# Second group norm's statistics from the spectrum, block by block, and the last tile's columns transformed by halves

## The chip, the cores and the metric

One core of a Trainium2 chip runs the whole program. The time is the device time of one execution in microseconds (us), and lower is better. The core has a matrix engine (PE, TensorE, with its weight loads listed as PEld), a vector engine (DVE), an activation engine (ACT, ScalarE), a general engine (POOL, GpSimd) and a sync engine (SP) that here issues all DMA transfers. Each engine works through its own instructions in order and waits on semaphores for the others.

## What is computed

The input x has shape (2, 48, 48, 768), all in 32-bit floats. Two layers with residuals are applied:

```python
x = x + attention(_gn(x), ...)      # layer 0: 12 heads, relative positions
x = x + spectral(_gn(x), ...)       # layer 1

def _gn(v, G=32, eps=1e-5):         # per image and per group of 24 channels
    g = v.reshape(B_, H_, W_, G, C_ // G)
    m = jnp.mean(g, axis=(1, 2, 4), keepdims=True)
    s = jnp.var(g, axis=(1, 2, 4), keepdims=True)
    return ((g - m) / jnp.sqrt(s + eps)).reshape(v.shape)

# layer 1
xf = jnp.fft.rfft2(x, axes=(1, 2), norm='ortho')
o1r, o1i = gelu(complex block-diagonal product of xf with w1, plus b1)  # 8 blocks of 96 channels
o2r, o2i = softshrink(complex block-diagonal product with w2, plus b2)
out = jnp.fft.irfft2(o2r + 1j * o2i, s=(H, W), axes=(1, 2), norm='ortho')
```

The change concerns the second `_gn`. Its mean only shifts the constant term of the transform, and its division by the deviation can be put into the rows of w1, because the transform is linear. The transform is orthonormal, so the sum of squares over the spectrum equals the sum of squares over the tokens; of a real input only 25 of 48 columns are kept, so the columns 1 to 23 count twice.

## The kernel before, in words

The two images (index b) are treated one after the other by the same code: first `attention`, then `project_out`, then `Spectral.run`. In the profiled execution `project_out` of the first image runs from about 1473 to 1662 us and its spectral part to about 1920 us; of the second image from about 3388 to 3580 us and to the end.

**Order of the work.** Inside attention, each engine's order is written out by hand (`InOrder`, which is why its lines appear as L67). In `project_out` and `Spectral` nothing is pinned: a scheduler lays out each engine's instructions ahead of the run. It takes the instruction that comes first in the code among those that it reckons to be ready, so an instruction from later code can stand before one from earlier code. On the chip each engine then keeps to that order.

**`project_out`** (L641). The result of attention lies in DRAM as oT. It is loaded three tiles of 128 tokens at a time (`Projection.tokens`, L623: one load of oT at L631, two loads of the softmax's inverses at L633 into one buffer `inv`, and one multiplication on POOL at L637). There are two buffers for the loaded group, so group g + 2 waits for the matmuls of group g. The residual x is loaded in six parts of 384 tokens (L653), and POOL adds the bias to each of their 24 rows (L655). For each of the 18 tiles t and each half hf of the 768 output channels, six matmuls (each shows as two instructions in the trace) fill one PSUM bank `acc` (L691), and DVE adds it to x in pieces (L700). PSUM has seven rotating banks for all of this.

`over_w(g)` (L663) transforms four finished image rows over the width: four matmuls (L671), four copies by ACT into the buffer y1 (L678, two buffers), and one transfer to DRAM `y_d` (L679). It is called for g up to 9 as the rows become complete and for g = 10 and 11 after the last tile.

`tile_stats` (L721) is called for each of 24 rows of 96 tokens: DVE sums each group (L724) and divides (L725), POOL subtracts the mean into `st_xc` (L727), ACT squares it (L730), DVE sums again (L731). `join_stats` (L734) joins the 24 results with eight DVE operations, two matmuls with a matrix of ones (L741 and L754) and a square root on ACT (L756).

**`Spectral`** (L763). `load` (L857) fetches from y_d one stretch of 192 channels in five pieces. `over_h(n)` (L867) transforms block n of 96 channels over the height: per piece five matmuls into a bank `ps_z` (L874) and a copy into z, alternately by DVE and ACT (L820, L822). `norm` (L796) picks each channel's mean and deviation out of `stats`; `scale` (L848) multiplies w1 of two blocks by 1/deviation (L853), and `constant` (L886) shifts one element of z per channel (L888). `first(n)` (L890) makes the first product, six groups of two matmuls (L899, L903), each followed by Gelu on ACT (L907). `second(n)` (L911) makes the second one: five pieces j of 20 matmuls (L926), each followed on DVE by the bias (L936) and the clipping (L942) and on POOL by the subtraction (L943). Every second block also transforms back over the height (`back_h`, L950, L957), and `back_w` (L974) transforms back over the width, adds to x2 (L989) and writes the output (L992). `run` (L996) calls, for each n: `over_h(n)`, then `second(n - 1)`, then `first(n)`.

Of the kernel before, what the change touches and what calls it, by code (L numbers as in the profile page):

```python
# [9 lines left out]
F32 = mybir.dt.float32  # L10
AF = mybir.ActivationFunctionType
ALU = mybir.AluOpType
AX = mybir.AxisListType
# [3 lines left out]
P = 128  # L17
HW = 48
# [622 lines left out]
def project_out(tc, k, x_b, pr, pools, y_d, x2, stats, constants):  # L641

    nc = tc.nc
    ps_b, small, work = pools
    bank = lambda name: ps_b.tile([P, 512], F32, tag="b", name=name)
    R = 2 * HW  # L650
    x_v = x_b.rearrange("(t p) c -> p t c", p=R)
    for i, part in enumerate(x2):
        nc.sync.dma_start(out=part, in_=x_v[:, i * XP : (i + 1) * XP, :])  # L653
        for j in range(XP):
            nc.gpsimd.tensor_tensor(part[:, j, :], part[:, j, :], pr.pb[:R], ALU.add)  # L655
        if i == 0:
            constants()
            pr.tokens(1)
    row = lambda hp: x2[hp // XP][:, hp % XP, :]
    local = small.tile([R, HW // 2, NG], F32, tag="local", name="local")  # L660
    dev = small.tile([R, HW // 2, NG], F32, tag="dev", name="dev")

    def over_w(g):  # L663

        y1 = work.tile([YP, 2, C], F32, tag="y1", name="y1")
        part = x2[2 * g // XP]
        t0 = 2 * g % XP
        for s in range(C // SC):
            ch = slice(s * SC, (s + 1) * SC)
            ps = bank("ps_y")  # L670
            nc.tensor.matmul(  # L671
                ps[:YP, : 2 * SC],
                lhsT=k.fw,
                rhs=part[:, t0 : t0 + 2, ch],
                start=True,
                stop=True,
            )
            nc.scalar.copy(y1[:, :, ch], ps[:YP, : 2 * SC].rearrange("p (t c) -> p t c", c=SC))  # L678
        nc.sync.dma_start(out=y_d[:, 2 * g : 2 * g + 2, :], in_=y1)  # L679

    done = turned = 0
    for t in range(NT):
        if t % 3 == 0:
            if t // 3 not in pr.o:
                pr.tokens(t // 3)
            o_sb = pr.o[t // 3]
        for hf in range(2):
            cols = slice(hf * UQ, (hf + 1) * UQ)
            acc = bank("acc")
            for cc in range(NCC):  # L690
                nc.tensor.matmul(  # L691
                    acc[:, :UQ],
                    lhsT=o_sb[:, cc, (t % 3) * P : (t % 3 + 1) * P],
                    rhs=pr.w[:, cc, cols],
                    start=(cc == 0),
                    stop=(cc == NCC - 1),
                )
            for p, hp, q, n in shifts(t):
                dst = row(hp)[q : q + n, cols]
                nc.vector.tensor_tensor(dst, acc[p : p + n, :UQ], dst, ALU.add)  # L700
        while (turned + 1) * 2 * R <= (t - 1) * P:
            over_w(turned)
            turned += 1
        while (done + 1) * R <= (t + 1) * P:
            tile_stats(
                nc,
                lambda name: work.tile([R, C], F32, tag="st", name=name),
                row(done),
                local[:, done, :],
                dev[:, done, :],  # L710
            )
            done += 1
    while turned < HW // 4:
        over_w(turned)
        turned += 1
    mean, rstd = join_stats(nc, k, small, bank, local, dev)
    nc.vector.tensor_copy(stats[:, 0, :], mean)
    nc.vector.tensor_copy(stats[:, 1, :], rstd)


def tile_stats(nc, work, xt, local, dev):  # L721

    x3 = xt.rearrange("p (g d) -> p g d", d=GC)
    nc.vector.tensor_reduce(local, x3, AX.X, ALU.add)  # L724
    nc.vector.tensor_scalar(local, local, 1.0 / GC, None, ALU.mult)  # L725
    xc = work("st_xc").rearrange("p (g d) -> p g d", d=GC)
    nc.gpsimd.tensor_tensor(  # L727
        xc, x3, local[:, :, None].to_broadcast([xt.shape[0], NG, GC]), ALU.subtract
    )
    nc.scalar.activation(xc, xc, AF.Square)  # L730
    nc.vector.tensor_reduce(dev, xc, AX.X, ALU.add)  # L731


def join_stats(nc, k, small, bank, local, dev):  # L734

    ntok = float(S)
    rows, tiles = local.shape[:2]
    part = small.tile([rows, NG], F32, tag="js_part", name="js_part")
    nc.vector.tensor_reduce(part, local.rearrange("p t g -> p g t"), AX.X, ALU.add)
    tot = bank("js_tot")  # L740
    nc.tensor.matmul(tot[:, :NG], lhsT=k.ones[:rows, :], rhs=part, start=True, stop=True)  # L741
    mean = small.tile([P, NG], F32, tag="js_mean", name="js_mean")
    nc.vector.tensor_scalar(mean, tot[:, :NG], 1.0 / ntok, None, ALU.mult)
    off = small.tile([rows, tiles, NG], F32, tag="js_off", name="js_off")
    nc.vector.tensor_tensor(
        off, local, mean[:rows, None, :].to_broadcast([rows, tiles, NG]), ALU.subtract
    )
    nc.vector.tensor_tensor(off, off, off, ALU.mult)
    nc.vector.tensor_scalar(off, off, float(GC), None, ALU.mult)
    nc.vector.tensor_tensor(off, off, dev, ALU.add)  # L750
    part2 = small.tile([rows, NG], F32, tag="js_part", name="js_part2")
    nc.vector.tensor_reduce(part2, off.rearrange("p t g -> p g t"), AX.X, ALU.add)
    tot2 = bank("js_tot2")
    nc.tensor.matmul(tot2[:, :NG], lhsT=k.ones[:rows, :], rhs=part2, start=True, stop=True)  # L754
    std = small.tile([P, NG], F32, tag="js_std", name="js_std")
    nc.scalar.activation(std, tot2[:, :NG], AF.Sqrt, bias=k.eps, scale=1.0 / (ntok * GC))  # L756
    rstd = small.tile([P, NG], F32, tag="js_rstd", name="js_rstd")
    nc.vector.reciprocal(rstd, std)
    return mean, rstd
# [3 lines left out]
class Spectral:  # L763

# [9 lines left out]
    def __init__(self, tc, k, a, pools, x2, y_d, out_b):  # L774
# [18 lines left out]
        nc.gpsimd.memset(self.o1[:, :, NF:], 0.0)  # L793
        self.y2, self.u2, self.w = {}, {}, {}

    def norm(self, stats):  # L796

        nc, cols = self.nc, []
        for i in range(2):
            m = self.small.tile([BS, NBK, 4], F32, tag="pick", name="pick")  # L800
            nc.vector.tensor_tensor(
                m,
                stats[:BS, i, :].rearrange("p (n g) -> p n g", g=4),
                self.k.gmask[:, None, :].to_broadcast([BS, NBK, 4]),
                ALU.mult,
            )
            c = self.small.tile([BS, NBK], F32, tag=f"col{i}", name=f"col{i}")
            nc.vector.tensor_reduce(c, m, AX.X, ALU.add)
            cols.append(c)
        self.rstd = cols[1]  # L810
        self.dc = self.small.tile([BS, NBK], F32, tag="dc", name="dc")
        nc.vector.tensor_scalar(self.dc, cols[0], -float(HW), None, ALU.mult)
# [35 lines left out]
    def scale(self, s):  # L848

        w = self.w[s][0]  # L850
        for i in range(NB):
            n = s * NB + i
            self.nc.vector.tensor_scalar(  # L853
                w[:, :, i, :], w[:, :, i, :], self.rstd[:, n : n + 1], None, ALU.mult
            )
# [11 lines left out]
    def over_h(self, n):  # L867

        nc, k, z = self.nc, self.k, self.z
        s, i = divmod(n, NB)  # L870
        for j in range(KW // WP):
# [13 lines left out]

    def constant(self, n):  # L886
        z0 = self.z[:, 0, 0, 0:1]
        self.nc.vector.tensor_tensor(z0, z0, self.dc[:, n : n + 1], ALU.add)  # L888
# [22 lines left out]
    def second(self, n):  # L911
# [8 lines left out]
        for j in range(KW // WP):  # L920
# [23 lines left out]
            if last and j > 1:  # L944
                self.back_h(j - 2)
        if last:
            self.back_h(j - 1)
            self.back_h(j)
# [47 lines left out]
    def run(self, stats):  # L996
# [4 lines left out]
        for n in range(NBK + 1):  # L1001
            s = n // NB
            more = n < NBK and s + 1 < NBK // NB
            if n < NBK:
                self.over_h(n)
                if n == 0:
                    self.norm(stats)
                if n % NB == 0:
                    self.scale(s)
                self.constant(n)  # L1010
                if more:
                    self.load(s + 1, pieces[:3] if n % NB == 0 else pieces[3:])
            if n:
                self.second(n - 1)
# [12 lines left out]
def block_kernel(tc, a, out):  # L1027
    nc = tc.nc
    B = a["x"].shape[0]
    with ExitStack() as ctx:  # L1030
# [20 lines left out]
        for b in range(B):  # L1051
            oT = dram.tile([C, S], F32, tag=f"oT{b}", name=f"oT{b}")
            y_d = dram.tile([YP, HW // 2, C], F32, tag=f"y_d{b}", name=f"y_d{b}")
            stats = cp.tile([P, 2, NG], F32, tag=f"stats{b}", name=f"stats{b}")
# [9 lines left out]
            with ExitStack() as ctx2:  # L1064
# [9 lines left out]
                constants = lambda: k.load(nc, a, small, {**fourier, "gmask": [BS, 4]})  # L1074
                with ExitStack() as ctx3:
                    work = ctx3.enter_context(tc.tile_pool(name="po_w", bufs=2))
                    pools = (ps_b, small, work)
                    project_out(
                        tc, k, a["x"][b], ready[0], pools, y_d, x2, stats, constants
# [11 lines left out]
                Spectral(tc, k, a, pools, x2, y_d, out[b]).run(stats)  # L1091


def shape_constants():
# [31 lines left out]
    gmask = np.arange(BS)[:, None] // GC == np.arange(4)[None, :]  # L1126
    group = np.arange(C // 2).reshape(3, P) // GC
    same = np.stack([group[j][:, None] == group[m][None, :] for j, m in SAME], 1) / GC
    named = {"same": same, "fh": fh, "fw": fw, "ih": ih, "iw": iw, "gmask": gmask}
# [50 lines left out]
```

## Time and profile before

Three runs took 3845.11, 3853.94 and 3853.54 us, a median of 3853.54 us. The profiled execution took 3845.32 us, of which its span from the first to the last instruction is 3843.2 us.

| engine | busy, us | share of the span | instructions |
|---|---|---|---|
| PE | 3661.7 | 95% | 31464 |
| DVE | 2950.0 | 77% | 6642 |
| ACT | 2502.4 | 65% | 3549 |
| POOL | 2063.9 | 54% | 646 |

| group touched by the change (both images) | count | mean ns of one |
|---|---|---|
| L724 DVE sum of x into local | 48 | 936 (first image's first eight: median) |
| L727 POOL x minus local into st_xc | 48 | 1481 |
| L730 ACT square of st_xc | 48 | 843 |
| L731 DVE sum of st_xc into dev | 48 | 949 (median) |
| L655 POOL bias into x | 48 | 1802 (median of the first image) |
| L888 DVE shift of one element of z | 16 | 155 |
| L853 DVE scaling of one block of w1 | 16 | 402 |

Times of the trace count from the start of the span. A busy time is an average over stages with different limits, so a change in one stage is read from that stage: from the gaps in PE's timeline, from what ended each gap, and from the chain of waits followed back from the end. PE's granted clock is the share of full speed that the chip lets it run at, and it is lower after a pause. Matmuls overlap in the records, so the distance from one to the next says more of their rate than the duration of one.

### The profile page before, as it was taken

Reading aid. Unit: us, or ns where it says so; the run is one execution under the profiler, and the core shown is the slowest. Engines: PE = TensorE matmul, PEld = TensorE weight load, DVE = VectorE, ACT = ScalarE, POOL = GpSimd, SP = SyncE. Lnnn points to the kernel's source line nnn. Section 1 sums busy time; section 2 is a strip of 40 time slices with the busy share of each in tenths; the row PEclk is TensorE's granted clock in tenths of the full one; section 3 lists DMA queues with packets and bytes.
Section 4 is the critical chain, followed back from the end, with each engine's and each line's share of the span. In section 5 each row is a group of like instructions: output and inputs, shape, how many; then the busy total and the mean of one; then the engine's idle time right before and its main releaser. Section 6 shows DMA issues by size and latency. Waiting matters only on the chain.

```text
span 3843.2 us, 83225 instructions
## 1 busy us (share of the span) xinstructions
PE 3661.7 (95%) x31464; PEld 2599.0 (68%) x31464; DVE 2950.0 (77%) x6642; ACT 2502.4 (65%) x3549; POOL 2063.9 (54%) x646
## 2 busy tenths in 40 slices
PE   8999999999999988989989999999999999779898
PEld 6677776767777655567566777777677776555675
DVE  4788888888889885654457988889888899846544
ACT  3688888888888882222137888888888888812221
POOL 2466666666666666321125666666666666663111
PEclk9999999999999999999989999999999999889899
DMA  3677777777777888434526777777777777884344
GB/s 100 143 174 169 173 171 167 175 165 178 167 171 171 172 195 199 126 90 119 165 83 138 172 174 169 174 167 174 168 174 168 173 170 168 202 195 114 90 119 133
DMA packets 496092, 606.92 MB, mean 158 GB/s; under 512 B 180109, under 2 KB 310797, under 8 KB 495694
## 3 DMA queue, kind: packets, MB, share of 16 engines
q1 hardware_dynamic: 495694, 601.61, 67.2%
q8 instruction: 250, 4.10, 0.5%
q14 instruction: 148, 1.21, 0.1%
HBM read 131.53 MB, written 87.67 MB: 57 GB/s over the span
## 4 chain that ended last, share of the span: by engine, by line
PE 81%; DMA 6%; DVE 5%; POOL 4%; SPq 2%; issue 1%; ACT 1%; POOLq 0%; DVEq 0%; ACTq 0%
PE ps_o L67 20%; PE ps_s L67 19%; PE ps_proj L67 14%; PE ps_v L67 8%; PE acc L691 5%; DVE s L67 4%; PE ps L926 4%; POOL s L340 3%; DMA pT<-s 2%; SPq L67 2%; PE ps_z L874 2%; PE ps_u L957 2%; PE ps_x L981 2%; PE ps L899 2%; PE ps L903 2%; PE ps_r L67 1%
## 5 line engine op out<-in xcount | busy, mean ns | idle before, releaser
L340 POOL TENSOR_TENSOR s<-rhw 128x2304 f32<-128x2304 f32 x432 | 1744.8, 4060 | 1152.1 <-DMA pT<-s 552.7
L67 DVE CUSTOM_DVE_ANT_0 s<-ps_s,s 128x512 f32<-128x512 f32 (+1 forms) x2160 | 1223.5, 633 | 372.9 <-issue 247.9
L67 ACT ACTIVATE s<-s,nm 128x1152 f32<-128x1152 f32 x864 | 1074.7, 1245 | 448.3 <-DVE nm L67 409.4
L67 DVE STREAM_TRANSPOSE s<-s 128x1152 f32<-128x1152 f32 x864 | 1111.8, 1344 | 5.5 <-ACT s L67 5.5
L67 ACT COPY pT<-s 32x1152 f32<-32x1152 f32 x864 | 993.3, 1150 | 24.5 <-PE ps_o L67 9.1
L67 PE MATMUL ps_o<-pT,v 128*64 128x128 f32 x15552 | 923.8, 279 | 70.8 <-DMA pT<-s 49.7
L67 PEld LDWEIGHTS ps_o<-pT,v 128*64 128x64 f32 x15552 | 872.0, 140 | 134.1 <-issue 66.1
L67 PE MATMUL ps_s<-kT,qT 64*128 64x512 f32 (+1 forms) x4320 | 918.2, 559 | 13.5 <-DVE mx L67 10.1
L67 PEld LDWEIGHTS ps_s<-kT,qT 64*128 64x128 f32 x4320 | 431.5, 187 | 449.7 <-issue 334.2
L67 PE MATMUL ps_proj<-xnT,w 128*128 128x384 f32 (+1 forms) x2016 | 600.2, 452 | 3.7 <-ACT gn_rstd L148 3.7
L67 PEld LDWEIGHTS ps_proj<-xnT,w 128*128 128x128 f32 x2016 | 362.4, 192 | 211.9 <-DVE mx L67 41.0
L691 PE MATMUL acc<-proj 128*128 128x384 f32 x864 | 292.0, 498 | 25.5 <-POOL proj L637 14.9
L67 PEld LDWEIGHTS ps_v<-w,xnT 128*128 128x128 f32 x2592 | 295.5, 193 | 21.5 <-DVE mx L67 21.5
L67 PE MATMUL ps_v<-w,xnT 128*128 128x128 f32 x2592 | 307.7, 279 | 0.0
L943 POOL TENSOR_TENSOR spectrum<-spectrum 128x480 f32<-128x480 f32 x80 | 96.3, 1204 | 325.8 <-DVE spectrum L942 322.1
L691 PEld LDWEIGHTS acc<-proj 128*128 128x128 f32 x864 | 168.4, 196 | 145.6 <-issue 20.4
L730 ACT ACTIVATE st_xc<-st_xc 96x768 f32<-96x768 f32 x48 | 40.5, 843 | 234.6 <-POOL st_xc L727 234.6
L67 DVE DVE_READ_ACCUMULATOR2_ANT mx<- 128x1 f32 x2160 | 179.4, 83 | 0.0
L700 DVE TENSOR_TENSOR x<-acc,x 32x384 f32<-32x384 f32 (+2 forms) x216 | 119.6, 553 | 77.6 <-PE acc L691 73.5
L67 ACT ACTIVATION_READ_ACCUMULATOR s<-s,nm 128x1 f32 x864 | 161.2, 187 | 0.0
L907 ACT ACTIVATE spectrum<-ps,b 96x400 f32<-96x400 f32 x96 | 56.5, 589 | 140.1 <-PE ps L903 140.1
L727 POOL TENSOR_TENSOR st_xc<-x,local 96x768 f32<-96x768 f32 x48 | 70.9, 1481 | 142.9 <-DVE local L725 120.9
(96 smaller groups left out, 2217.8 us busy)
## 6 DMA issues: line engine op xcount, KB each, us to landing
pT<-s SPq DMA_DIRECT2D x2592, 144.0 KB
t<-rel SPq DMA_DIRECT2D x144, 189.0 KB
rhw<-t SPq DMA_DIRECT2D x144, 144.0 KB
y_d<-y SPq DMA_DIRECT2D x24, 672.0 KB
y<-y_d SPq DMA_DIRECT2D x40, 360.0 KB
u_d<-spectrum SPq DMA_DIRECT2D x40, 360.0 KB
u<-u_d SPq DMA_DIRECT2D x48, 300.0 KB
xt<-in_x SPq DMA_DIRECT2D x12, 1152.0 KB
```

The costliest lines, as they stand in the source:

```text
L67: return lambda *args, **kw: self.tc.keep_in_program_order(op(*args, **kw))
L340: nc.gpsimd.tensor_tensor(s[:, h, :].rearrange("p (y x) -> p y x", x=HW), rhw[:, x, h, :HW][:, :, None].to_broadcast([P, HW, HW]), rhw[:, ...
L691: nc.tensor.matmul(acc[:, :UQ], lhsT=o_sb[:, cc, (t % 3) * P : (t % 3 + 1) * P], rhs=pr.w[:, cc, cols], start=(cc == 0), stop=(cc == NCC - 1),
L700: nc.vector.tensor_tensor(dst, acc[p : p + n, :UQ], dst, ALU.add)
L727: nc.gpsimd.tensor_tensor(xc, x3, local[:, :, None].to_broadcast([xt.shape[0], NG, GC]), ALU.subtract)
L874: nc.tensor.matmul(ps[:BS, w * 96 : (w + 1) * 96], lhsT=self.y2[s, j][:, w, i * BS : (i + 1) * BS], rhs=k.fh, start=True, stop=True,)
L899: nc.tensor.matmul(ps[:BS, :400], lhsT=w1[:, wa, i, :], rhs=zf[:, 0, fs], start=True, stop=False,)
L903: nc.tensor.matmul(ps[:BS, :400], lhsT=w1[:, wb, i, :], rhs=zf[:, 1, fs], start=False, stop=True,)
L926: nc.tensor.matmul(ps[64 * r : 64 * r + 64, w * BS : (w + 1) * BS], lhsT=self.o1[:, ri, f0 : f0 + 64], rhs=w2[:, (0, 2, 1, 0)[2 * r + ri], ...
L943: nc.gpsimd.tensor_tensor(val, val, clip, ALU.subtract)
L957: nc.tensor.matmul(ps[: 2 * HW, :480], lhsT=k.ih, rhs=d2[:, c0 : c0 + 480], start=True, stop=True)
L981: nc.tensor.matmul(ps[: 2 * HW, : 2 * SC], lhsT=k.iw, rhs=self.u2[s, i][:, t : t + 2, :], start=True, stop=True,)
```

## The change

- `tile_stats`, `join_stats`, the buffers local, dev and stats, and the old `norm`, `scale` and `constant` are taken out, and with them the square root on ACT.
- In `over_h(n)`, ACT squares each of the five pieces of z as it is copied and sums the squares into one column of `power` per piece. The sum covers the columns of the spectrum 1 to 23.
- `mean()`: one matmul of the constant term with a matrix `gmean`, which averages the 24 channels of a group, then DVE subtracts this from the constant term, and ACT squares and sums the columns 0 and 24.
- `norm(n)`: DVE joins the six sums, one matmul with `gmean` averages them over the group, and DVE forms 1/sqrt by an integer first guess and three Newton steps, eleven operations on a column of 96 after the one that reads the matmul, and scales w1 of block n.
- `mean` and `norm` of block n are called inside `second(n - 1)`, after its pieces 0 and 2; for n = 0 they stand between `over_h(0)` and `first(0)`.
- For the last tile of `project_out`, the rows that are still to be transformed over the width are transformed for channels 0 to 383 after the first half of the tile's output and for channels 384 to 767 after the second half, each with a y1 buffer and a transfer of its own.

```diff
-    def over_w(g):
+    def over_w(g, steps=range(C // SC)):
         y1 = work.tile([YP, 2, C], F32, tag="y1", name="y1")
...
-        for s in range(C // SC):
+        for s in steps:
...
-        nc.sync.dma_start(out=y_d[:, 2 * g : 2 * g + 2, :], in_=y1)
+        ch = slice(steps[0] * SC, (steps[-1] + 1) * SC)
+        nc.sync.dma_start(out=y_d[:, 2 * g : 2 * g + 2, ch], in_=y1[:, :, ch])
...
                 nc.vector.tensor_tensor(dst, acc[p : p + n, :UQ], dst, ALU.add)
-        while (turned + 1) * 2 * R <= (t - 1) * P:
+            if t == NT - 1:
+                half = C // SC // 2
+                for g in range(turned, HW // 4):
+                    over_w(g, range(hf * half, (hf + 1) * half))
+        while t < NT - 1 and (turned + 1) * 2 * R <= (t - 1) * P:
             over_w(turned)
             turned += 1
-        while (done + 1) * R <= (t + 1) * P:
-            tile_stats(
...
-    while turned < HW // 4:
-        over_w(turned)
-        turned += 1
-    mean, rstd = join_stats(nc, k, small, bank, local, dev)
-    nc.vector.tensor_copy(stats[:, 0, :], mean)
-    nc.vector.tensor_copy(stats[:, 1, :], rstd)
...
+    def square(self, part, total):
+        r, w, h = part.shape[1:]
+        junk = self.junk[:, : r * w * h].rearrange("p (r w h) -> p r w h", r=r, h=h)
+        self.nc.scalar.activation(junk, part, AF.Square, accum_out=total)
...
+    def mean(self):
+        nc, z0 = self.nc, self.z[:, 0, 0, 0:1]
+        mean = self.bank("ps_nm")
+        nc.tensor.matmul(mean[:BS, :1], lhsT=self.k.gmean, rhs=z0, start=True, stop=True)
+        nc.vector.tensor_tensor(z0, z0, mean[:BS, :1], ALU.subtract)
+        self.square(self.z[:, :, :: KW - 1, :], self.power[:, KW // WP :])
+
+    def norm(self, n):
+        nc = self.nc
+        s, i = divmod(n, NB)
+        pieces = KW // WP
+        total, var, rstd, fit = (self.column(f"nm_{c}") for c in ("total", "var", "rstd", "fit"))
+        nc.vector.tensor_reduce(total, self.power[:, :pieces], AX.X, ALU.add)
+        nc.vector.scalar_tensor_tensor(
+            total, total, 2.0, self.power[:, pieces:], ALU.mult, ALU.add
+        )
+        ps = self.bank("ps_nv")
+        nc.tensor.matmul(ps[:BS, :1], lhsT=self.k.gmean, rhs=total, start=True, stop=True)
+        nc.vector.tensor_scalar(var, ps[:BS, :1], 1.0 / S, GN_EPS, ALU.mult, ALU.add)
+
+        bits = rstd.bitcast(I32)
+        nc.vector.tensor_scalar(bits, var.bitcast(I32), 1, None, ALU.arith_shift_right)
+        nc.vector.tensor_scalar(bits, bits, -1, 0x5F3759DF, ALU.mult, ALU.add)
+        for _ in range(3):
+            nc.vector.tensor_scalar(fit, rstd, rstd, var, ALU.mult, ALU.mult)
+            nc.vector.tensor_scalar(fit, fit, -0.5, 1.5, ALU.mult, ALU.add)
+            nc.vector.tensor_tensor(rstd, rstd, fit, ALU.mult)
         w = self.w[s][0]
-        for i in range(NB):
-            n = s * NB + i
-            self.nc.vector.tensor_scalar(
-                w[:, :, i, :], w[:, :, i, :], self.rstd[:, n : n + 1], None, ALU.mult
-            )
+        nc.vector.tensor_scalar(w[:, :, i, :], w[:, :, i, :], rstd, None, ALU.mult)
...
     def over_h(self, n):
...
                 ps[:BS, :480].rearrange("p (w r h) -> p w r h", r=2, h=HW),
             )
+            w0, w1 = max(j * WP, 1), min((j + 1) * WP, KW - 1)
+            self.square(z[:, :, w0:w1, :], self.power[:, j : j + 1])
...
-    def second(self, n):
+    def second(self, n, more):
...
             nc.gpsimd.tensor_tensor(val, val, clip, ALU.subtract)
             if last and j > 1:
                 self.back_h(j - 2)
+            if more and j == 0:
+                self.mean()
+            if more and j == 2:
+                self.norm(n + 1)
...
                 self.over_h(n)
-                if n == 0:
-                    self.norm(stats)
-                if n % NB == 0:
-                    self.scale(s)
-                self.constant(n)
...
             if n:
-                self.second(n - 1)
+                self.second(n - 1, n < NBK)
+            else:
+                self.mean()
+                self.norm(n)
```

## The prediction

> **What bounds the kernel.** I read the busy table first, then PE's clock, PE's timeline through both stages that the change touches, the other engines there, and the chain of waits.
>
> ```profile
> PE 3661.7 (95%) x31464; PEld 2599.0 (68%) x31464; DVE 2950.0 (77%) x6642; ACT 2502.4 (65%) x3549; POOL 2063.9 (54%) x646
> ```
>
> PE is the bound nearly everywhere, so work taken off DVE, ACT or POOL pays only where PE stood still for it. The projection of the first image shows this (PE's timeline, then POOL's, then SP's: start, length, what, and in brackets the idle time before it):
>
> ```profile
> 1516.88 4.04 PE L691 MATMUL acc<-proj 128*128 128x384 f32 x12
> 1529.60 7.04 PE L691 MATMUL acc<-proj 128*128 128x384 f32 x12 [8.68 <-DVE x L700]
> 1541.57 8.77 PE L691 MATMUL acc<-proj 128*128 128x384 f32 x20 [4.93 <-POOL proj L637]
> ```
>
> ```profile
> 1507.19 2.92 POOL L727 TENSOR_TENSOR st_xc<-x,local 96x768 f32<-96x768 f32 x2
> 1510.08 14.15 POOL L655 TENSOR_TENSOR x<-x,proj 96x768 f32<-96x768 f32 x8
> 1536.48 5.04 POOL L637 TENSOR_TENSOR proj<-proj 128x2304 f32<-128x2304 f32 x1 [1.88 <-DMA proj<-inv_d]
> ```
>
> ```profile
> 1528.28 0.30 SPq L679 DMA_DIRECT2D y_d<-y  x1
> 1528.63 0.58 SPq L633 DMA_DIRECT2D proj<-inv_d  x1
> ```
>
> PE waits for tile 6 (L691 at 1541.57). Behind it stands a ring: DVE's L725 writes `local` only as late as 1524.26, POOL's st_xc follows, ACT's square follows that, ACT's copies of y stand behind the square, y_d's issue waits for them, and behind y_d in SP's queue stands the load of inverses that tile 6 needs. At a steady 7.74 us for a tile and 2.58 us for an over_w (chain rows), 432 and 96 instructions are 139.3 + 31.0 = 170.3 us; from 1473.0 to 1662.6 is 189.6, so 19.3 are lost, and 21.8 in the second image (3388.3 to 3580.5).
>
> The second place is the end of that stage, in the chain:
>
> ```profile
> 1657.44 3.88 PE ps_y L671 x12
> ...
> 1663.27 1.49 POOL st_xc L727
> 1664.78 0.84 ACT st_xc L730
> 1666.01 3.79 DMA y_d<-y
> 1669.94 3.89 DMA y<-y_d
> 1673.97 6.98 PE ps_z L874 x50
> ```
>
> The last copy of y stands behind two squares; then come a write and a read. After that PE is full: per block 4.25 us of ps_z, 8.40 of L926, 8.07 of L899/L903 (12 by 0.67), 8.5 of ps_u in every second.
>
> **Part A, the statistics leave the projection (gain).** Without st_xc, POOL has 24 rows at 1.77 = 42.6 us and the products at 5.06. First image: part 0 ends 1480.8, product 1 about 1488, five parts by 1523.5 (35.5 us). PE reaches tile 6 at 1473.0 + 6 x 7.74 + 2 x 2.58 = 1524.6. If the inverses keep their place behind the second y_d, that is issued about 1518 (over_w ends 1516.9, copies 0.65 after), lands 7.7 later (chain row), and the product ends 1531: tile 6 comes 10.5 us sooner. If POOL alone decides, 1528.5 or 13.1 sooner. In the second image the same sums give 3448.4 and 3444 against 3459.0: 10.6 and 15. The restart gains 1 to 2 more, as its pause shrinks (24 instructions took 10.06 there, 7.74 when steady). I take 14 each, **-28 us**; bounds -22 and -34.
>
> **Part B, halves of the last tile (gain).** PE's matmuls stay the same. Counted from the last tile's start (1649.54), the copies of the first half's last row end about 11.0 (first half 3.87, row 10 1.29, second half 3.87, row 11 1.29, last copy 0.6) instead of 16.5. Write and read still follow, so ps_z could start 5 us sooner. Unknown: whether the load of channels 0 to 191 waits for the write of 384 to 767 too, which with two y1 buffers ends about when today's does: 0 gain. I take 4 each, nearer to the first since only other columns are written: **-8**, bounds 0 and -10. join_stats' eight operations end with it; they ran beside these transfers (L853 starts 1673.40, ps_z 1673.97), so they give nothing of their own.
>
> **Part C, norm of block 0 (loss).** Nothing stood between ps_z and L899; now a chain does. The price of a small dependent DVE operation is read off this row of steps:
>
> ```profile
> 1672.69 0.18 DVE L718 COPY stats<-js_rstd 128x32 f32<-128x32 f32 x1
> 1672.90 0.19 DVE L801 TENSOR_TENSOR pick<-stats,gmask 96x32 f32<-96x32 f32 x1
> 1673.12 0.18 DVE L808 TENSOR_REDUCE col<-pick 96x8 f32<-96x32 f32 x1
> ```
>
> That is 0.21 from start to start. Chain: copy 0.65 and 0.1 of wait, square of 480 about 0.64 (between L907's 0.589 for 400 and L730's 0.843 for 768), accumulator read 0.19, second square 0.5, two sums 0.33, matmul and its reader 0.69 (js_part's end 1663.32 to js_mean's end 1664.01), eleven operations 2.3, w1 0.40, wait 0.1: 5.9 us. Can PE fill it? The order lets later code go ahead when it is ready: DVE's L717 stands between L748 and L749, which come earlier and depend on each other, and POOL's L845 of the spectral part runs at 1541. over_h(1) has its data (same load) and needs five of seven banks, so I expect its 4.25 us in the gap. Rest 1.65, and about 1.35 of slow clock: 3.0 each, **+6**. Unfilled: 5.9 + 1.8 = 7.7 each, +15.4; filled and warm +4.
>
> Row against rule: after gaps of 8.68 and 4.93 us, the clock granted from 1530 to 1546 was 0.61 and the 24 instructions took 2.3 us longer. The Trainium skill ("TensorE: Matmul & The Clock Gate", "Part 1: The HAM clock gate") says that an idle window of about 3.4 us halves the clock until about 3.4 us of busy time have passed. By it, an estimate, an unfilled gap costs 1.7 us more, at most 3.4; it speaks against a chain of this length, and the sum would move by under 3.
>
> **Part D, blocks 1 to 7 (loss).** Added per block on PE: two one-column matmuls of two instructions. ps_z's 96-column ones go at 4.25/50 = 0.085, js_tot's pair took 0.41 cold; so 0.17 to 0.41 each. I take 0.17: 16 blocks x 2 = **+5.4**, bounds 5 and 13. On ACT five squares and one small one, some 4.6 us a block, beside 3.5 of Gelu and 2.5 of copies in 20.7: covered, but copies of z slip about 1 us. On DVE 14 small operations, between L936 and L942, which take 1.31 of every 1.68 us: some three get in per piece. Block 1, counted from second(0)'s start: squares end at 3.4, the sums at 4.3, the variance's matmul at 4.8, then seven operations in pieces 2 to 4 and the rest after: w1 is ready at about 11, first(1) wants it at 8.4, 2.65 late. Behind first(1) on PE stands over_h(2), which can again go ahead; in the blocks with back_h the window is 17 us, and only ps_u of piece 4 loses up to 1 us (it waits for L943, slack 0.8 today). PE also stands in order behind the variance's matmul if ACT is later than planned. A second price shows in DVE's timeline and in POOL's of the spectral part:
>
> ```profile
> 1514.04 10.22 DVE L725 TENSOR_SCALAR local<-local 96x32 f32<-96x32 f32 x1
> ```
>
> ```profile
> 1698.18 1.21 POOL L943 TENSOR_TENSOR spectrum<-spectrum 128x480 f32<-128x480 f32 x1 [0.44 <-DVE spectrum L942]
> ```
>
> L725 needs 0.18 and took 10.22, to the end of POOL's run of L655 (1524.23): some DVE operations can't run beside a busy POOL. L942 does (0.65 throughout). Which of the 14 can't, no row tells. The chain passes some four L943 (pieces 1 to 4), each busy 1.21 of 1.68 us, and would wait 0.6 at a mean: 4 x 0.72 x 0.6 = 1.7 more. Bounds 0 and 4.4 per block; I take 0.9 x 14 = **+12.6**, nearer to nothing since PE's gaps were 6 in 184 us there and over_h can fill 4.25.
>
> Row against rule: the Trainium skill ("SBUF — State Buffer", "Who interferes with whom") says that a DVE operation with two SBUF inputs, or one that uses two ports for one input, waits for the whole of a GpSimd operation that reads SBUF. L725 is the second kind and agrees; by the rule the three Newton products and the joining sum are the first kind, which no row here shows beside POOL. This speaks against the change: if all of it fell on PE (14 x 1.7 = 23.8 in place of 12.6), the sum would be about -1.
>
> If Gelu and Square needed different tables, each block would pay two loads of 1.28 (L907's row); Square at L730 followed Exp without one, so I leave it out.
>
> **Sum.** -28 - 8 + 6 + 5.4 + 12.6 = -12.0. The profiled execution took 3845.3 (span 3843.2 and 2.1 around it), at the lower end of the runs; the median is 8.2 above. I add 4 for that: 3837.
>
> **Rivals.**
> 1. *The chain is a new wait in every block* (slower): w1 comes late through DVE's order and POOL's hold. C unfilled, and 3 us in each of 14: -28 - 8 + 15.4 + 5.4 + 42 = +26.8, 3876. For it: PE keeps to its order, DVE is 78% full in `second`, L725's wait. Against: over_h of the next block is free to move. It decides from 1.1 us per block on, with C unfilled.
> 2. *The projection's wait is replaced* (no change): POOL's 24 rows and the loads of L631 and L633 keep tile 6 late, A -14, and the load waits for all columns, B 0: -14 + 6 + 5.4 + 12.6 = +10, 3859. For it: POOL ends close to PE's need, and L633 took 7.7 and 9.8 us to land. Against: the ring above is gone.
> 3. *Everything is covered*: A -34, B -10, C +4, D 5.4: -34.6, 3815.
>
> **Chances.** Forecast 0.50 (its own range 3820 to 3850), rival 1 0.18, rival 2 0.15, rival 3 0.17. About 0.3% (11.5 us, so 3842 and 3865) can be told from no change. Faster: rival 3 and three quarters of the forecast, 0.55; same: rival 2 and the rest, 0.27; slower 0.18. Range 3814 to 3872: half of rival 3 and two thirds of rival 1 are left out.
>
> **What would show it.** A: PE's gap before tile 6 at most 6 us, nothing on POOL between L655 and L637. B: y_d's last write of the first half 5 us before the second's and the load right behind it. C: ps_z x100 before the first L899. D: PE's gaps before L899 and behind the variance's matmul under 1 us, and the Newton steps at 0.2 each. Wrong if L899 waits for w1 in most blocks, if the Newton steps last as long as L943, if ACT loads tables in every block, or if tile 6 still waits 10 us.

## The result, and the profile after

The changed kernel is 0.7% slower: 3877.35 us, median of four runs (3875.79 to 3880.72), against 3853.74 for the kernel before, a ratio of 1.0071 [1.0058, 1.0085]. The profiled execution took 3880.72 us (span 3878.9), 35.4 more than the profiled one of before; that one lay at the lower end of its runs and this one at the upper, so the medians differ by only 23.6.

In the changed kernel L689 is the projection's matmul, L654 and L638 POOL's bias and inverse products, L675/L677 the copies and transfers of y. L839 is ps_z, L862/L866 the first product (L899/L903 before), L890 the second. L793 and L808 are the matmuls of mean and variance, L804 joins the sums, L817 is the product at the end of each Newton step, L819 scales w1, and L907 is POOL's subtraction (L943 before).

The busy table of the changed kernel:

```profile
PE 3678.3 (95%) x31520; PEld 2605.8 (67%) x31520; DVE 2843.9 (73%) x6692; ACT 2518.4 (65%) x3689; POOL 1993.1 (51%) x598
```

DVE lost 106 us and POOL 71 us of work, and the kernel is slower all the same; PE's time rose by 16.6 with only 56 more instructions. Where the time went is read from PE's timeline, cut at the same events in both traces (first and second image, us):

| stretch of PE | before | after | change, sum | predicted |
|---|---|---|---|---|
| A: first acc to the last tile's start | 176.5, 179.1 | 166.8, 166.2 | -22.6 | -28 |
| B: from there to the end of block 0's ps_z | 31.4, 33.6 | 26.5, 25.6 | -12.9 | -8 |
| C: from there to the end of first(0), with that product's slow start | 7.9, 9.5 | 16.3, 16.5 | +15.4 | +6 |
| D: rest, to the end of the last back_w but one | 214.2, 212.9 | 236.3, 236.4 | +45.6 | +18 |
| attention (+6.5), and from the wait ahead of the last back_w on (+3.5) | | | +10.0 | 0 |

The rows make 35.5 of the spans' 35.7. The gain came, and parts C and D spent it nearly twice over: 61.0 against 35.5. The +10 of the last row lies in code that the change doesn't touch. Attention's 6.5 is best read as a difference between executions: over all eleven traces, whose attention is the same, the first projection starts anywhere from 1471.2 to 1477.1 us. The wait ahead of the first image's last back_w is not: it is 5.3 us before and 8.0 after, and 8.0 to 9.3 in all the variants below that keep the new chain where the change has it or nearly so, 5.7 to 6.2 in the others; its cause was not looked into. Parts C and D are seen in PE's timeline of the changed kernel (start, length, what, and in brackets the idle time before it with what ended it):

```profile
1667.05 3.45 PE L839 MATMUL ps_z<-fh,y 96*96 96x96 f32 x20 [3.47 <-DMA y<-y_d]
1672.63 0.48 PE L808 MATMUL ps_nv<-nm_total,gmean 96*96 96x1 f32 x2 [1.97 <-DVE nm_total L804]
1676.60 1.62 PE L862 MATMUL ps<-spectrum,w 96*96 96x400 f32 x2 [3.48 <-DVE w L819]
...
1686.79 4.41 PE L839 MATMUL ps_z<-fh,y 96*96 96x96 f32 x50
...
1693.19 3.52 PE L890 MATMUL ps<-w,spectrum 96*64 96x96 f32 x80
1696.64 0.33 PE L808 MATMUL ps_nv<-nm_total,gmean 96*96 96x1 f32 x2
1696.90 3.52 PE L890 MATMUL ps<-w,spectrum 96*64 96x96 f32 x80
1703.81 0.88 PE L862 MATMUL ps<-spectrum,w 96*96 96x400 f32 x2 [3.38 <-DVE w L819]
1704.53 1.36 PE L866 MATMUL ps<-spectrum,w 96*96 96x400 f32 x2
...
1713.61 4.41 PE L839 MATMUL ps_z<-fh,y 96*96 96x96 f32 x50
```

In the kernel before, first(1) follows the second product without a wait:

```profile
1701.59 0.91 PE L899 MATMUL ps<-spectrum,w 96*96 96x400 f32 x2
```

The first three lines are block 0: 1.97 + 3.48 us of waiting, and ps_z of block 1 comes only behind first(0), at 1686.79. The others are block 1: PE finishes the second product and stands 3.38 us for w1; ps_z of block 2 stays behind first(1), at 1713.61, where the code has it. The next L866 takes 1.36 us, and the windows of PE say why (stretch, us, busy time with counts for PE, PEld, DVE, ACT, POOL, then the granted clock):

```profile
1704.00:1709.00 5.00, 5.00 (x11) 2.19 (x11) 0.21 (x1) 1.15 (x2) 1.20 (x1) 0.66 0.00 0
```

The granted clock was 0.66 for these 5 us; it was 0.56 from 1760 to 1767, in block 3. The wait repeats in blocks 1, 3, 5 and 7 of both images, eight times (2.20 to 3.38 us); in six of them the product behind it is slow. Blocks 2, 4 and 6 follow a `second` with back_h in it, and there w1 is ready in time.

DVE's timeline shows what makes w1 late:

```profile
1694.54 0.16 DVE L804 SCALAR_TENSOR_TENSOR nm_total<-nm_total,power 96x1 f32<-96x1 f32 x1
...
1698.94 0.53 DVE L817 TENSOR_TENSOR nm_rstd<-nm_rstd,nm_fit 96x1 f32<-96x1 f32 x1
...
1700.89 1.20 DVE L817 TENSOR_TENSOR nm_rstd<-nm_rstd,nm_fit 96x1 f32<-96x1 f32 x1
...
1702.61 0.15 DVE L817 TENSOR_TENSOR nm_rstd<-nm_rstd,nm_fit 96x1 f32<-96x1 f32 x1
...
1703.26 0.41 DVE L819 TENSOR_SCALAR w<-w,nm_rstd 96x288 f32<-96x288 f32 x1
```

```profile
1700.88 1.19 POOL L907 TENSOR_TENSOR spectrum<-spectrum 128x480 f32<-128x480 f32 x1 [1.42 <-DVE nm_fit L816]
```

The sums are done at 1694.70, but PE takes the variance's matmul only at 1696.64, after piece 2, where the code has it: 2 us lost. Then the same product on a column of 96 takes 0.15 us with POOL idle, 0.53, and 1.20 while POOL's L907 (the second fence, POOL's timeline) runs from 1700.88 to 1702.07. This is the hold that the prediction weighed as a rule of the Trainium skill ("SBUF — State Buffer", "Who interferes with whom") and could not see in any row for such a product: the trace agrees, and the 48 products took 16.0 us instead of 48 x 0.15 = 7.2.

### The profile page after: what moved, and what is told of

Same layout as the page of the kernel before. It is cut to its first block, busy times and chain, and to the rows that moved or that the text cites. A ratio compares the mean times of both kernels' runs of the same rounds, so it can differ in the third digit from the quotient of the medians.

```text
span 3878.9 us, 83414 instructions
## 1 busy us (share of the span) xinstructions
PE 3678.3 (95%) x31520; PEld 2605.8 (67%) x31520; DVE 2843.9 (73%) x6692; ACT 2518.4 (65%) x3689; POOL 1993.1 (51%) x598
## 5 line engine op out<-in xcount | busy, mean ns | idle before, releaser
L68 PEld LDWEIGHTS ps_v<-w,xnT 128*128 128x128 f32 x2592 | 295.8, 193 | 21.2 <-DVE mx L68 21.2
L689 PE MATMUL acc<-proj 128*128 128x384 f32 x864 | 288.3, 493 | 12.5 <-POOL proj L638 12.5
L907 POOL TENSOR_TENSOR spectrum<-spectrum 128x480 f32<-128x480 f32 x80 | 96.2, 1202 | 370.3 <-DVE nm_total L804 185.7
L689 PEld LDWEIGHTS acc<-proj 128*128 128x128 f32 x864 | 166.4, 193 | 130.1 <-POOL proj L638 13.7
L675 ACT COPY y<-ps_y 112x384 f32<-112x384 f32 x96 | 46.0, 479 | 318.7 <-PE ps_y L668 286.1
L890 PE MATMUL ps<-w,spectrum 96*64 96x96 f32 x3200 | 144.4, 248 | 0.8 <-issue 0.8
```

The lines of the kernel that those rows point to most:

```text
L68: return lambda *args, **kw: self.tc.keep_in_program_order(op(*args, **kw))
L689: nc.tensor.matmul(acc[:, :UQ], lhsT=o_sb[:, cc, (t % 3) * P : (t % 3 + 1) * P], rhs=pr.w[:, cc, cols], start=(cc == 0), stop=(cc == NCC - 1),
L890: nc.tensor.matmul(ps[64 * r : 64 * r + 64, w * BS : (w + 1) * BS], lhsT=self.o1[:, ri, f0 : f0 + 64], rhs=w2[:, (0, 2, 1, 0)[2 * r + ri], ...
L907: nc.gpsimd.tensor_tensor(val, val, clip, ALU.subtract)
```

## The experiments

Each kernel below was timed next to the kernel before on its own chip; the stretches come from each one's trace. The first three ask for the cause of part D, the next three for the clock and for part B, the last three for a version that keeps the gain.

**Take the wait away.** w1 is multiplied by a constant column of ones; the chain runs in full, but nobody waits for its end. So this kernel leaves out the division by the deviation.

```diff
-        nc.vector.tensor_scalar(w[:, :, i, :], w[:, :, i, :], rstd, None, ALU.mult)
+        nc.vector.tensor_scalar(
+            w[:, :, i, :], w[:, :, i, :], self.k.ones[:BS, 0:1], None, ALU.mult
+        )
```

> Left out: w1 is multiplied by a column of ones instead of 1/deviation, so the output is not normalised; every square, matmul and Newton step is still made, but the first product of a block no longer waits for them. Theory 'wait': the loss is PE's wait for the scaled w1 (30 us over both images in the changed kernel's profile) and the slow clock of the matmuls behind each wait (18 us), so the time falls by 44 to 50 us to about 3830, under the kernel before. Rival 'work': the added squares, small vector operations and matmuls cost the time by themselves, so it falls by less than 15 us, to 3862 or more.

Measured: 3834.98 us against 3850.04, ratio 0.9966 [0.9953, 0.9979]: by the ratios 1.05% or some 40 us less than the changed kernel, a little under the 44 to 50 of the first theory, with the same operations on every engine but without the wait. The group of the first product (count, busy us, mean ns of one, idle time before it and what ended that), first in the changed kernel, then here:

```profile
L862 PE MATMUL ps<-spectrum,w 96*96 96x400 f32 x192 | 90.4, 555 | 29.9 <-DVE w L819 29.9
```

```profile
L862 PE MATMUL ps<-spectrum,w 96*96 96x400 f32 x192 | 83.8, 519 | 0.0
```

All 29.9 us of waiting are gone, and the matmuls are shorter as well. The loss is the wait for w1 and what follows from it. The added work costs far less: without the wait, the stretch from the start of `second` to first(n) is still mostly 0.82 us longer than before in the odd blocks and 0.50 in the others, some 10 us over both images.

**Take POOL's hold away.** The Newton product gets its second factor as a scalar operand and so has one tensor input.

```diff
-            nc.vector.tensor_tensor(rstd, rstd, fit, ALU.mult)
+            nc.vector.tensor_scalar(rstd, rstd, fit, None, ALU.mult)
```

> The third Newton operation is a product with a scalar operand instead of a product of two tensors; same result. Theory 'hold': these 48 products took 16.0 us instead of 7.2 because a product of two SBUF tensors waits for the POOL subtraction that runs then; none will take over 0.3 us now, w1 is ready about 1 us sooner in the eight odd blocks, and the time falls by 8 to 15 us, to 3862 to 3869 (some waits become too short to slow the clock). Rival 'order': the chain is late because of where it stands in the vector engine's order; the products get shorter, the vector engine then waits for the next bank instead, and the time stays within 4 us of 3877.

Measured: 3871.19 us, ratio 1.0057 [1.0042, 1.0072], some 6 less than the changed kernel by the medians, between what the two theories gave; the two intervals overlap, so the rows below say more than the total. The group of the product:

```profile
L817 DVE TENSOR_SCALAR nm_rstd<-nm_rstd,nm_fit 96x1 f32<-96x1 f32 x48 | 9.9, 206 | 1.0
```

The mean fell from 334 to 206 ns and none took over 210, so this form is not held. But the eight waits only fell from 23.3 to 21.2 us in all, 2.6 each. Most of the rest is the clock: with gaps a little shorter, five of the eight first products behind them ran in 8.1 to 8.2 us, where two did in the changed kernel; all eight took 71.4 us instead of 77.6. The hold is real and a small part of the wait; the shorter gaps may have saved the clock's part by chance, as the last section shows.

**Start the chain one piece earlier.** The variance and the Newton steps are called after piece 1.

```diff
-            if more and j == 2:
+            if more and j == 1:
```

> The variance and Newton steps of the next block are called after piece 1 of the second product instead of after piece 2, nothing else. Theory 'order': the variance's matmul moves 1.7 us forward on PE (one piece of 20 matmuls), the wait for w1 in the odd blocks falls from about 3 to 1.3 us, 8 x 1.7 = 13.6 us, and with clock the time is 3855 to 3865. Rival 'sums late': the squares on ACT end so late that the variance's matmul now holds PE up inside the second product, by about 1 us per block, and the time is 3870 or more.

Measured: 3854.22 us, ratio 1.0007 [0.9997, 1.0016], 23 less than the changed kernel and no slower than the one before; the gain is a little more than was expected. PE's timeline of block 1 and the windows of the same kernel:

```profile
1692.23 0.33 PE L808 MATMUL ps_nv<-nm_total,gmean 96*96 96x1 f32 x2
1692.49 5.17 PE L890 MATMUL ps<-w,spectrum 96*64 96x96 f32 x120
1699.34 0.88 PE L862 MATMUL ps<-spectrum,w 96*96 96x400 f32 x2 [1.68 <-DVE w L819]
```

```profile
1699.00:1704.00 5.00, 4.66 (x14) 2.36 (x15) 1.96 (x4) 1.56 (x3) 2.40 (x2) 1.00 0.00 0
```

The matmul now stands ahead of piece 2, three pieces (x120) follow it instead of two, and the wait is halved here; the eight waits fell from 23.3 to 8.8 us in all. A gap of 1.68 us leaves the clock at 1.00, and the slow product behind it is gone too, in all eight blocks. POOL's hold even grew (mean of the product 498 ns), which shows again that it is not what decides. The place of the variance's matmul on PE does.

**Keep the clock up.** The wait stays, but PE runs four 384-column matmuls, whose result nothing reads, ahead of each first product that waits.

```diff
+    def warm(self):
+        ps = self.bank("ps_w")
+        for _ in range(4):
+            self.nc.tensor.matmul(
+                ps[: 2 * HW, : 2 * SC], lhsT=self.k.ih[: 2 * HW], rhs=self.x2[0][:, :2, :SC],
+                start=True, stop=True, skip_group_check=True,
+            )
...
+            if n < NBK and (n == 0 or n % NB):
+                self.warm()
```

> Before the first product of blocks 0, 1, 3, 5 and 7, PE makes four extra matmuls of 384 columns (2.6 us) whose result nobody reads; all else as changed. Theory 'clock': the ten waits for w1 themselves stay (30 us, of which the extra matmuls now fill 26), but PE does not cool down, so the first product no longer runs slow (18 us over both images, less where the wait is longer than 2.6) and the time falls by 10 to 18 us, to 3859 to 3867. Rival 'the price is the wait alone': the slow first products have another cause (their banks, Gelu), and the time stays within 4 us of 3877 or rises.

Measured: 3864.54 us, ratio 1.0043 [1.0023, 1.0062], some 13 less than the changed kernel by the medians and 11 by the ratios, though PE does more. PE's timeline in block 1:

```profile
1695.91 2.82 PE L878 MATMUL ps_w<-x,ih 96*96 96x384 f32 x8
1699.28 0.91 PE L862 MATMUL ps<-spectrum,w 96*96 96x400 f32 x2 [0.55 <-DVE w L819]
```

w1 comes no sooner, but all sixteen first products, block 0's too, take 8.1 to 8.2 us from start to start of what follows. In the changed kernel eight odd blocks took 77.6 against 65.3 before: 12.3 us of the loss are the clock after the gap and not the gap.

**The halves, each way.** First the changed kernel with the last tile's columns transformed as before:

```diff
-            if t == NT - 1:
-                half = C // SC // 2
-                for g in range(turned, HW // 4):
-                    over_w(g, range(hf * half, (hf + 1) * half))
-        while t < NT - 1 and (turned + 1) * 2 * R <= (t - 1) * P:
+        while (turned + 1) * 2 * R <= (t - 1) * P:
...
+    while turned < HW // 4:
+        over_w(turned)
+        turned += 1
```

> The last tile's columns are transformed for all channels at the end again, the rest as changed. Theory: of the 5 to 8 us per image by which block 0's transform ends sooner after the last tile's start, part comes from the squares that no longer stand before ACT's copies, part from the halves; undoing the halves costs 2 to 5 us per image, 3881 to 3887. Rival 'hidden': the load of the later pieces waits for the second half's writes in SP's queue anyway, and the time stays within 3 us of 3877.

Measured: 3882.02 us, ratio 1.0088 [1.0071, 1.0104]. ps_z starts 21.7 us after the last tile's start instead of 15.6, but the first product only 3.6 and 2.8 later: with halves, ps_z starts early and then stands 3.47 us for the rest of the data (the first line of PE's timeline above). So the halves are worth 3.2 us an image by these rows and 2.3 by the medians, whose intervals overlap. Then the kernel before with the same halves and nothing else; the statistics stay as they were:

```diff
+            if t == NT - 1:
+                half = C // SC // 2
+                for g in range(turned, HW // 4):
+                    over_w(g, range(hf * half, (hf + 1) * half))
...
-    while turned < HW // 4:
-        over_w(turned)
-        turned += 1
```

> The kernel before with the halves of the last tile alone; statistics from tokens stay. Theory: block 0's transform ends 2 to 5 us sooner per image, 4 to 10 in all, 3840 to 3846 where the kernel before takes 3850. Rival: ACT's copies stand behind the squares of the last rows and join_stats ends only then, so nothing moves: within 3 us of the kernel before.

Measured: 3848.10 us, ratio 0.9998 [0.9988, 1.0007], no gain. PE's timeline of this kernel:

```profile
1675.25 0.61 PE L756 MATMUL js_tot<-js_part,ones 96*128 96x32 f32 x2 [7.30 <-DVE dc L814]
1675.67 6.28 PE L876 MATMUL ps_z<-fh,y 96*96 96x96 f32 x50
```

`join_stats` becomes the wait: PE stands 7.30 us ahead of its last matmul, with ps_z behind it. That matmul starts 25.7 us after the last tile's start, 21.8 in the kernel before: the tile's second half, which the statistics need, now stands behind transforms of the first half. The halves pay only once the statistics of the tokens are gone.

**Write the code so that PE has work during the chain.** z gets a second buffer, over_h(n + 1) is written ahead of second(n - 1) and first(n), and the mean and variance of block n + 2 are called in second(n), a whole block before they are wanted; w1 is scaled after piece 0. The Newton product has the scalar operand here too.

```diff
+            if n == 0:
+                self.over_h(0)
...
+                self.mean(0)
+                self.norm(0)
+                self.scale(0)
+            if n + 1 < NBK:
+                self.over_h(n + 1)
...
-                self.second(n - 1, n < NBK)
+                self.second(n - 1, n < NBK, n + 1 < NBK)
...
+            if ahead and j == 0:
+                self.scale(n + 1)
...
-                self.norm(n + 1)
+                self.norm(n + 2)
```

> The transform over the height runs one block ahead with two buffers for z, mean and norm of a block are made during the block before, its w1 is scaled one block later, and the Newton product takes a scalar operand. All work stays. Theory 'wait': every block's chain has a whole block as cover, only block 0 still waits about 2 us, so the time falls by 40 to 50 us, to 3827 to 3837, under the kernel before (3854). Rival 'work': it falls by less than 15 us, and new gaps of PE appear behind the copies of z or the banks.

Measured: 3834.73 us, ratio 0.9958 [0.9941, 0.9975]. PE's timeline:

```profile
1669.90 0.48 PE L814 MATMUL ps_nv<-nm_total,gmean 96*96 96x1 f32 x2 [1.97 <-DVE nm_total L810]
1670.24 6.73 PE L849 MATMUL ps_z<-fh,y 96*96 96x96 f32 x50
1676.81 0.84 PE L872 MATMUL ps<-spectrum,w 96*96 96x400 f32 x2
```

ps_z of block 1 now fills the gap of block 0, and no first product waits any more. What the prediction expected of the scheduler comes true when the code is written in that order and z has two buffers; which of the two was needed was not tried apart. The rest of part C, 1.97 us in front of the variance, stays.

**The rest of part A.** In the changed kernel tile 6 still waits. PE's, POOL's and SP's timelines:

```profile
1535.34 10.73 PE L689 MATMUL acc<-proj 128*128 128x384 f32 x24 [6.43 <-POOL proj L638]
```

```profile
1494.95 35.35 POOL L654 TENSOR_TENSOR x<-x,proj 96x768 f32<-96x768 f32 x20 [0.78 <-DMA x<-in_x]
1530.22 5.07 POOL L638 TENSOR_TENSOR proj<-proj 128x2304 f32<-128x2304 f32 x1
```

```profile
1521.72 0.30 SPq L677 DMA_DIRECT2D y_d<-y  x1
1522.07 0.58 SPq L634 DMA_DIRECT2D proj<-inv_d  x1
```

The product stands behind 20 bias rows without a gap, and it also needs the inverses, whose load stands behind a y_d on SP; 1522.07 and the load's 7.7 us (before) make 1529.8, and POOL ends its rows at 1530.3. Two candidates end within 0.5 us of each other. So the kernel written ahead got POOL's order by hand, with the bias rows of the last two of six parts after the product:

```diff
+    def add_bias(part):
+        for j in range(XP):
+            InOrder(tc, nc.gpsimd).tensor_tensor(part[:, j, :], part[:, j, :], pr.pb[:R], ALU.add)
...
-            nc.gpsimd.tensor_tensor(part[:, j, :], part[:, j, :], pr.pb[:R], ALU.add)
+        if i < 4:
+            add_bias(part)
...
+            if t == 6:
+                for part in x2[4:]:
+                    add_bias(part)
```

> The version with the transform one block ahead, and POOL's order in the projection written out: the product of group 2 comes before the bias rows of parts 4 and 5. Theory 'POOL': tile 6 waits 6.4 us per image because that product stands behind all 24 bias rows; it now comes as soon as its inverses have landed, 4 to 6 us sooner with 1 to 2 us of slow clock, and the time falls from 3835 to 3821 to 3829. Rival 'inverses': the second load of inverses stands behind y_d's second write in SP's queue and lands no earlier, so tile 6 waits as long and the time stays within 4 us of 3835.

Measured: 3834.67 us, ratio 0.9963 [0.995, 0.9976], no gain. POOL's timeline:

```profile
1524.55 5.03 POOL L68 TENSOR_TENSOR proj<-proj 128x2304 f32<-128x2304 f32 x1 [13.65 <-DMA w<-in_w]
```

POOL is free 13.65 us early and waits for a load, tile 6 still waits 6.03 us. The name of the load is that of the last one seen; going by the times it is the inverses', issued at 1516.76, directly behind a y_d at 1516.40, and 7.8 us under way when the product starts. Last, the same kernel with each group loaded three tiles sooner, so that its loads stand ahead of that y_d, and the late bias rows moved along:

```diff
+            if 3 <= t < NT - 3:
+                pr.tokens(t // 3 + 1)
+            if t == 3:
-            if t == 6:
                 for part in x2[4:]:
                     add_bias(part)
```

> As the last version (one block ahead, POOL's order written out), and each group of the projection after the second is loaded one group earlier in the code, so that its inverses stand before the writes of y in SP's queue. Theory 'inverses': the product of group 2 then follows the bias rows of part 3 at once, tile 6 no longer waits (6 us and 2 to 3 of slow clock per image), and the time falls from 3835 to 3816 to 3822. Rival 'x parts': the residual's last parts or the loads of oT land too late, the wait goes to another tile, and the time stays within 5 us of 3835.

Measured: 3820.36 us (3817.94 to 3822.51), ratio 0.9923 [0.9907, 0.994], the fastest of all and 0.8% under the kernel before. PE's timeline at tile 6:

```profile
1527.65 8.01 PE L700 MATMUL acc<-proj 128*128 128x384 f32 x24 [0.38 <-POOL proj L68]
```

The wait is 0.38 us here and 1.43 in the second image, and the 24 matmuls take 8.01 us instead of 10.73.

## Why the prediction was wrong

The forecast was 3837 and faster; 3877.35 lies above the range. Rival 1 gave 3876 by the right mechanism, though with another spread: not 3 us in each of 14 blocks, but 2.2 to 3.4 in eight, with a slow clock behind most of them. That its total comes so close is luck: its part A was 5.4 too good and its part B 4.9 too poor, and 10 us of the measured difference lie outside all its terms. Of the signs of being wrong one came: the first product waits for w1 in ten of the sixteen blocks. ACT loads one table for the spectral part of each image.

- **Part A: right in kind, a little small (-22.6 for -28, inside its bounds).** The ring of statistics, copies and y_d is gone, and tile 6 of the first image starts 58.2 us after the first matmul of the projection instead of 68.6: 10.4 sooner, where its first case had 10.5 and the sum 14. The inverses kept their place behind a y_d, as that case assumed, and POOL's rows end at nearly the same time: changing POOL's order alone gave nothing, changing it and the place of the load 14 us. The gain of 1 to 2 us for a faster restart did not come: the 24 matmuls of tile 6 took 10.73 us, 10.06 before.
- **Part B: -12.9 for -8.** Its term for the halves was a little large (6.4 by the rows and 4.7 by the medians when they are taken out, 8 predicted; they also make PE wait 1.05 and 1.15 us for DVE between the two rows' transforms, which the sum left out). Its sentence that join_stats gives nothing of its own was wrong: with the halves alone that chain takes the place of the transfers, so the halves gain only because it is gone. Without the halves the stretch is still 6.3 us shorter than before (30.1 and 28.6): that is what the statistics' leaving gave. The unknown it named was settled for the better: the load of the first channels is issued at 1655.29, ahead of the second half's writes at 1657.61 and 1660.27, and ps_z starts at 1659.56.
- **Part C: +15.4 for +6, the unfilled bound of 15.4.** The chain's length was right: 6.1 and 5.8 us from the end of ps_z to the first product, for 5.9. Over_h(1) did not go ahead. The product behind the gap took 2.1 and 2.6 us longer than 8.06, where the bound had 1.8; in the second image 1.6 of that was there before the change, so the match is in part luck.
- **Part D: +45.6 for +18, the step that decided.** By terms: the one-column matmuls 0.82 us in the odd blocks and 0.50 in the others (read where nobody waits for w1) for 0.34, so 9.6 for 5.4; waits 23.3 in eight blocks and the slow clock behind them 12.3, together 35.6 for 12.6. The remaining 0.5 us are not assigned. Its estimate that first(1) comes 2.65 us late was near to the 3.38 that was measured in both images; discounting it to 0.9 was not. Its ground for that, "PE's gaps were 6 in 184 us there", says nothing of a wait that the change adds, and the figure is off: from 1680 to 1864 us PE was busy for 184.00 of 184.00 us before.

**The step that failed** is one in both parts: "over_h(1) has its data … so I expect its 4.25 us in the gap" and "over_h(2), which can again go ahead". Its evidence was an instruction of DVE and one of POOL that stood ahead of earlier code. PE's own rows showed nothing of the kind before, and after the change its matmuls keep to the order of the code in all blocks, ps_z of the next block behind the waiting first product of this one. Removing the wait gave 40 us back, and writing over_h ahead in the code took all waits for w1 away. Why the scheduler did not move the matmuls by itself stays open.

**A price that was left out:** the slow clock after a gap was put into part C (1.35 us for each), but not into part D, where eight gaps cost 12.3. The hold by POOL was in the sum through a mean of 0.6 us per pass and is real, but taking it away shortened the waits by only 2.1 of 23.3.

## What to carry to other kernels

When a new chain is put ahead of the bounding engine's work, look for evidence in that engine's own timeline before counting on later work to fill the gap: another engine's reordering says nothing of it. Where it keeps to the code's order, write the filling work ahead of the wait in the code (with a buffer of its own), and call each matmul of the chain where its operand is ready, not a piece later. A stage that loses a wait should be followed to the next thing in the queue: here a load behind a store on SP and POOL's own order both held what the change had set free, and moving both took another 14 us off, where POOL's order alone gave nothing.

## What the runs showed of the hardware

- **The price of a short gap isn't steady.** With the variance after piece 1, gaps of 1.06 to 1.68 us before the first product cost it nothing (8.1 to 8.2 us, as with no gap). In the changed kernel, gaps of 2.2 to 3.4 us cost 0, 1.7 or up to 2.9 us more, and the length alone does not decide: three gaps of 2.84 were followed by 8.11, 9.90 and 11.11. With the scalar operand, five gaps of 2.56 to 2.79 us left the product at 8.1 to 8.2, and three of 2.63 made it 9.80, 9.80 and 11.14. The Trainium skill ("TensorE: Matmul & The Clock Gate", "Part 1: The HAM clock gate") speaks of a window of about 3.4 us; shorter gaps than that were enough here, some of the time.
- **Useless matmuls can shorten a kernel.** Eight matmul instructions that nothing reads, put into each of ten gaps that had to be waited out anyway, saved 11 to 13 us.
- **The form of an operation decides whether POOL holds it.** The same product on 96 x 1 took up to 1.20 us beside a POOL operation with two tensor inputs, and never over 0.21 with its second factor as a scalar operand.
